# Cross-attention stack on one core: order of the first loads, first q and k by halves, y's statistics ahead of q's scaling, and an earlier folding of v's bias

## Chip, core and metric

The kernel runs on one core of one Trainium2 chip. The metric is the time of one execution in microseconds (us) of the device; a lower time is better. A profile is one execution taken with the hardware profiler; its times count from the first instruction (the span's start).

## What is computed

Sixteen batches of 256 tokens by 256 features (x), with a context y of the same size, go through three attention layers and an MLP, all in float32, with 16 heads of 16 features. Layer 0 is a cross-attention with RMS norms, layer 1 a causal self-attention with rotary embedding, layer 2 a cross-attention with rotary embedding.

```python
# layer 0
q_norm = rmsnorm(query, g_q); c_norm = rmsnorm(context, g_c)
Q = (q_norm @ Wq); K = (c_norm @ Wk); V = (c_norm @ Wv)      # by heads
attn = softmax(where(mask, Q @ K.T * scale, -inf))
x = rmsnorm(query + (attn @ V) @ Wo, g_out)
# layer 1: h = ln(x); q, k rotated; causal; v = h @ sa_wv + sa_bv; x = x + (a @ sa_wo + sa_bo)
# layer 2: q from ln(x), k and v from y;                       x = x + (a @ ca_wo + ca_bo)
# MLP
return x + (gelu(ln(x) @ fc1_w + fc1_b) @ fc2_w + fc2_b)
```

## The kernel before, in words

There are 48 attentions, three layers for each of 16 batches, in the order that `ORDER` lists: the first five are layer 0 of batches 0 to 4. Each attention has four blocks of scores (three in the causal layer): `scores` (L476) makes a block of K times Q in two PSUM tiles `S`, ScalarE takes exp (L487) out of them into `pt`, and `values` (L515) multiplies by V into the one PSUM tile `A` one block later. The preparation of later attentions (statistics, norm, turn, q, k, v) and the finishing of earlier ones (invert, divide, project) is laid between these blocks by hand: everything inside `tc.manual_schedule()` runs in the order in which it is written, on each engine's own queue. What is emitted ahead of that (the memsets, and the two products on zeros at L171) is placed by the framework.

Norms of layer 0 are not applied to the inputs. The gains are multiplied into the weights once (`fold_gain`, L230, on VectorE), x's scale is multiplied into q, and y's scale goes into exp (as `sy`, L343) and into v. `stats_x` and `stats_y` make them: squares with a running sum on VectorE (L246), then two steps on GpSimd (L238, L239). x's scale rx is needed along the free axis; for the first two attentions `spread` (L358) does this by eight small products with the identity, and ScalarE copies the result to `rq` (L363). `q` of layer 0 (L294, then L421) multiplies the product by rq and by a parity column, once for even and once for odd heads, into `qm`. `k` (L294) is copied by ScalarE (L437) to `kT`; `v` (L307) goes out through VectorE (L448) with y's scale and the mask.

Inputs come by DMAs, issued from two queues. SP's takes x's rows, x transposed, y transposed and y's rows of batch 0 (`load_x`, `load_y`), then the mask, batches 1 and 2, and further on all other weights. ACT's takes the vector of small parameters `vec` and then layer 0's Wq, Wk, Wv and Wo. Each of these tiles is 256 KB.

PSUM has eight banks: two tiles S of two banks, one tile A, and three tiles d (`dense_ps`) for all other products.

`fold_v` (L219, L226) makes the product of layer 1's norm bias with its v weights, 16 passes on TensorE, and adds it on VectorE to v's bias row. It and `fold_bias` (L189), the same for q and k and the MLP, stand at the end of the second attention (i == 1, n == 3). The two products on zeros (L171) need only the identity and a zeroed tile, and nothing reads their result.

Of the kernel before, what the change touches and what calls it, by code (L numbers as in the profile page):

```python
# [8 lines left out]
F32 = mybir.dt.float32  # L9
# [3 lines left out]
ALU = mybir.AluOpType  # L13
AX = mybir.AxisListType

P = 128
B, S, D = 16, 256, 256
# [3 lines left out]
KC = D // P  # L21
# [25 lines left out]
def xattn_kernel(  # L47
# [21 lines left out]
    nc = tc.nc  # L69
# [5 lines left out]
    def ctile(shape, name, dtype=F32):  # L75
        return const.tile(shape, dtype, tag=name, name=name)
# [8 lines left out]
    def rows_of(b):  # L85
        return cur[:, NC * b : NC * b + NC, :]
# [4 lines left out]
    yTs = {}  # L91

    def load_x(b):
        nc.sync.dma_start(out=rows_of(b), in_=x[b].rearrange("(c p) d -> p c d", p=P))
        xTs[b] = work.tile([P, KC, S], F32, tag="xT", name=f"xT{b}", bufs=3)
        nc.sync.dma_start(out=xTs[b], in_=xt[b].rearrange("(k p) s -> p k s", p=P))

    def load_y(b):
        yTs[b] = work.tile([P, KC, S], F32, tag="yT", name=f"yT{b}", bufs=Y_LIVE)
        nc.sync.dma_start(out=yTs[b], in_=yt[b].rearrange("(k p) s -> p k s", p=P))  # L100
        ys[b] = work.tile([P, NC, D], F32, tag="y", name=f"y{b}", bufs=3)
        nc.sync.dma_start(out=ys[b], in_=y[b].rearrange("(c p) d -> p c d", p=P))
# [5 lines left out]
    def load_w(t, aps, eng):  # L108
        at = 0
        for a in aps:  # L110
            m = a.shape[1]
            eng.dma_start(out=t[:, :, at : at + m], in_=a.rearrange("(k p) n -> p k n", p=P))
            at += m

    vec = ctile([P, NVEC + 2], "vec")
    nc.scalar.dma_start(out=vec, in_=vecs)
    load_x(0)
    w0_sb = ctile([P, KC, 3 * D], "w0")
    load_w(w0_sb, w0, nc.scalar)
    load_y(0)  # L120
    mask_u8 = ctile([P, B * NC], "mask_u8", U8)
    nc.sync.dma_start(out=mask_u8, in_=mask)
    load(1)
# [36 lines left out]
    def dense_ps():  # L160
        return psD.tile([P, 512], F32, tag="d", name="d")
# [4 lines left out]
        pads.append([ctile([P, 32], f"pad{i}_{j}") for j in range(2)])  # L166
        nc.gpsimd.memset(pads[i][0], 0.0)

    idle = dense_ps()
    for n in range(2):  # L170
        nc.tensor.matmul(  # L171
            idle, lhsT=ident, rhs=firsts[0].rearrange("p t s -> p (t s)"), start=True, stop=True
# [55 lines left out]
    def fold_gain(w, cols, vcol, chunks=range(KC)):  # L228
        for k in chunks:
            nc.vector.tensor_scalar(  # L230
                w[:, k, cols], w[:, k, cols], vec[:, vcol + k : vcol + k + 1], None, ALU.mult
            )
# [52 lines left out]
        )  # L285


    def by_feature(src, w, at):

        ps = dense_ps()  # L290
        for t in range(KC):
            for k in range(KC):
                for j in range(0, P, 32):
                    nc.tensor.matmul(  # L294
                        ps[j : j + 32, t * S : (t + 1) * S],
                        lhsT=w[:, k, at + t * P + j : at + t * P + j + 32], rhs=src[:, k, :],
                        start=(k == 0), stop=(k == KC - 1), skip_group_check=True,
                    )
        return ps.rearrange("p (t s) -> p t s", s=S)
# [15 lines left out]
    class Att:  # L315
# [36 lines left out]
        def spread(self):  # L352

            self.rq = work.tile([P, S], F32, tag="rq", name="rq")
            ps = dense_ps()
            for c in range(NC):
                for j in range(0, P, 32):
                    nc.tensor.matmul(  # L358
                        ps[j : j + 32, c * P : (c + 1) * P],
                        lhsT=self.rx[:, c : c + 1].to_broadcast([P, 32]), rhs=ident,  # L360
                        start=True, stop=True, skip_group_check=True,
                    )
            nc.scalar.copy(self.rq, ps[:, :S])  # L363
# [51 lines left out]
        def q(self):  # L415
            ps = by_feature(self.hT, self.w, 0)
            self.qm = work.tile([P, KC, 2, S], F32, tag="qm", name="qm", bufs=2)
            if self.layer == 0:
                rq = self.rq.unsqueeze(1).to_broadcast([P, KC, S])
                for i in range(2):  # L420
                    nc.vector.scalar_tensor_tensor(  # L421
                        self.qm[:, :, i, :], ps, parity[i], rq, ALU.mult, ALU.mult
                    )
                return
            a, u = self.rotated(ps, 0)
            nc.vector.tensor_tensor(a, a, u, ALU.add)
            for i in range(2):
                nc.vector.tensor_scalar(self.qm[:, :, i, :], a, parity[i], None, ALU.mult)

        def k(self):  # L430
            ps = by_feature(self.kvT, self.w, D)
# [164 lines left out]
    def do(i, *names):  # L596
        a = att(i)
        for name in names:
            if a is not None:
                getattr(a, name)()  # L600
# [242 lines left out]
    combined = combine()  # L843

    with tc.manual_schedule():
        do(0, "stats_x")
        fold_gain(w0_sb, slice(0, D), V_GQ)
        fold_gain(w0_sb, slice(D, 2 * D), V_GC)
        do(0, "turn", "spread", "q", "k", "stats_y")
        fold_gain(w0_sb, slice(2 * D, 3 * D), V_GC)  # L850
        nc.vector.tensor_copy(mask01, mask_u8)
        for va in vas:
# [9 lines left out]
        for i in range(N_ATT):  # L862
            a, last = att(i), att(i - 1)
            ahead = att(i + 3)
            if i > 1 and ahead is not None and ahead.layer == 0:
                load(ahead.b)

            finishing = i >= 3 and att(i - 3).layer == 0  # L870
            for n in range(len(a.blocks)):
                if n == 0 and a.causal and not finishing:
                    do(i + 2, "stats")
                a.scores(n)
                if n > 0:
                    a.values(n - 1)
                elif last is not None:
                    last.values(-1)
                final = len(a.blocks) - 1
                if n == 0:  # L880
                    if i == 0:
                        a.v()
                        do(1, "spread")
                    do(i - 3, "finish")
                    if finishing or not a.causal:
                        do(i + 2, "stats")
                    do(i - 2, "divide")
                    if not finishing:
                        do(i + 2, "norm")
                    do(i + 1, "q")  # L890
                elif n == 1:
                    do(i + 1, "k")
                    if finishing:
                        do(i + 2, "norm")
                    for j in kept.get(i, ()):
                        att(j).keep()
                if n == final - 1:
                    do(i + 1, "v")
                    do(i - 1, "invert")
                    do(i + 2, "send")  # L900
                if n == final:
                    do(i - 2, "project")
                    do(i + 2, "turn", "receive")
                if i == 0 and n == 0:
                    load(4)
                    nc.sync.dma_start(out=bias_sb, in_=rows.partition_broadcast(P))
                    nc.sync.dma_start(out=turn_sb, in_=turn)
                if i == 0 and n == 1:
                    load_w(ca_sb, ca, nc.sync)
                if i == 0 and n == 2:  # L910
                    load_w(fc1_sb, [fc1], nc.sync)
                if i == 1 and n == 0:
                    load_w(sao_sb, [sa_o], nc.sync)
                    load_w(cao_sb, [ca_o], nc.sync)
                if i == 1 and n == 2:
                    load_w(fc2_sb, [fc2], nc.sync)
                    nc.sync.dma_start(
                        out=rope_sb, in_=rope.rearrange("(c p) t d -> p c t d", p=P)
                    )
                if i == 1 and n == 3:  # L920
                    cols = fold_bias()
                    fold_v()
                if i == 2 and n == 3:
                    fold_gain(sa_sb, slice(0, 3 * D), V_G1)
                if i == 3 and n == 3:
                    fold_cols(cols)
                    fold_gain(ca_sb, slice(0, D), V_G2)
                if i in (6, 8) and n == 3:
                    fold_gain(fc1_sb, slice(0, FF), V_G3, [i // 8])
                if n == 1 and i > 8 and not a.causal:  # L930
                    next(combined, None)
                if i == N_ATT - 2 and n == 1:
                    mlps[0].stats()
                    mlps[0].norm()
                if i == N_ATT - 1 and n == 2:
                    mlps[0].turn()
                    mlps[0].mix()
                if i == N_ATT - 1 and n == 3:
                    mlps[1].stats()
                    mlps[1].norm()  # L940
# [472 lines left out]
```

## Time and profile before

| | |
|---|---|
| runs, us | 950.59, 950.79, 953.49; median 950.79 |
| the profiled execution, us | 953.16 |
| its span, us | 951.4 |
| TensorE (PE) busy | 936.1 us, 98% of the span |
| VectorE (DVE) busy | 666.0 us, 70% |
| ScalarE (ACT) busy | 571.9 us, 60% |
| GpSimd (POOL) busy | 294.6 us, 31% |
| DMA | 46.96 MB, 49 GB/s over the span, 333 GB/s from 2 to 12 us |

A busy TensorE is not one at its peak, since matmuls are pipelined and their ends are modelled. In the profile a float32 product shows as two passes, so 16 products are 32 instructions. A wait is put down to what ended last; time of an engine that waits costs something only where it lies in the chain of work that ended last.

### The profile page before, as it was taken

The page shows a single profiled execution, that of the slowest core. Times are in us where ns is not written, and L with a number is a line of the kernel's source. Part 1 is how long each engine was busy: PE and PEld are TensorE (multiplying, and loading weights), DVE is VectorE, ACT ScalarE, POOL GpSimd, SP SyncE. Part 2 cuts the span into 40 slices and gives each one's busy share as a digit, 9 for nine tenths or more (in the row PEclk, how much of TensorE's full clock was granted, in tenths as well). Part 3 has the DMA queues.
Part 4 walks back from the last instruction along what each step waited for, and adds up shares of the span by engine and source line. Part 5 has one row for each costly group of instructions (what it writes and reads, how often), then busy time and mean ns, then how long its engine had stood idle before and what let it go on. Part 6 is the DMA issues. An engine that isn't in the chain of part 4 may idle for free.

```text
span 951.4 us, 30022 instructions
## 1 busy us (share of the span) xinstructions
PE 936.1 (98%) x12374; PEld 551.6 (58%) x12374; DVE 666.0 (70%) x1483; ACT 571.9 (60%) x821; POOL 294.6 (31%) x502
## 2 busy tenths in 40 slices
PE   8999999999999999999999999999999899999997
PEld 4444455445454545455454445445445699999997
DVE  4347768877776797677866768787776776667653
ACT  4666666766666766666766676666676634444440
POOL 4213454334334344144242423334112211222200
PEclk9999999999999999999999999999999999999999
DMA  9531221202121122110222101010101000000001
GB/s 316 171 97 29 78 71 32 71 18 79 25 70 28 42 54 73 24 33 19 72 71 74 32 22 27 19 29 21 26 21 26 13 24 23 13 12 23 23 24 47
DMA packets 66089, 46.96 MB, mean 49 GB/s; under 512 B 25364, under 2 KB 65044, under 8 KB 65944
## 3 DMA queue, kind: packets, MB, share of 16 engines
q1 hardware_dynamic: 64712, 43.89, 16.8%
q8 instruction: 100, 1.64, 0.7%
q10 hardware_dynamic: 1232, 1.07, 0.4%
q14 instruction: 45, 0.37, 0.1%
HBM read 26.54 MB, written 5.79 MB: 34 GB/s over the span
## 4 chain that ended last, share of the span: by engine, by line
PE 88%; DVE 5%; DMA 3%; POOL 1%; ACT 1%; issue 1%; SPq 0%; DVEq 0%; POOLq 0%
PE S L476 18%; PE A L515 17%; PE d L294 16%; PE d L307 15%; PE A L762 6%; PE upX L676 6%; PE downZ L762 3%; PE upZ L676 3%; PE d L274 2%; PE d L762 2%; PE d L676 1%; DMA hop<-av 1%; DVE a L410 1%; PE d L657 1%; DVE u L410 1%
## 5 line engine op out<-in xcount | busy, mean ns | idle before, releaser
L487 ACT ACTIVATE pt<-S 128x1024 f32<-128x1024 f32 x224 | 217.4, 1022 | 114.3 <-PE S L476 114.3
L476 PE MATMUL S<-qm,kT 32*128 32x512 f32 (+1 forms) x1536 | 202.9, 600 | 2.1 <-DVE kT L435 1.0
L515 PE MATMUL A<-pt,va 128*32 128x256 f32 (+1 forms) x3072 | 193.0, 367 | 1.3 <-POOL pt L494 0.8
L515 PEld LDWEIGHTS A<-pt,va 128*32 128x32 f32 x3072 | 80.5, 109 | 158.5 <-issue 95.4
L487 ACT ACTIVATE pt<-S,sy 128x1024 f32<-128x1024 f32 x128 | 135.7, 1111 | 46.1 <-PE S L476 44.0
L555 POOL TENSOR_TENSOR seen<-seen,sums 128x64 f32<-128x64 f32 x48 | 15.4, 320 | 280.4 <-DVE sums L554 185.8
L476 PEld LDWEIGHTS S<-qm,kT 32*128 32x128 f32 x1536 | 62.4, 183 | 68.5 <-issue 25.4
L494 POOL TENSOR_SCALAR_AFFINE_SELECT pt<-pt 128x512 f32<-128x512 f32 x128 | 88.5, 713 | 27.4 <-ACT pt L487 27.3
L283 POOL TENSOR_TENSOR cur<-cur,bias 128x512 f32<-128x512 f32 x48 | 65.3, 1365 | 58.9 <-DVE xn L263 58.9
L402 ACT ACTIVATE a<-d,qk_bias 128x256 f32<-128x256 f32 x128 | 53.8, 471 | 38.5 <-PE d L294 33.4
L294 PE MATMUL d<-hT,sa 128*32 128x256 f32 x1024 | 63.1, 379 | 0.0
L238 POOL TENSOR_SCALAR r_ln<-bmv 128x2 f32<-128x2 f32 x48 | 12.6, 261 | 153.3 <-DVE bmv L257 152.6
L529 ACT COPY av<-A 128x512 f32<-128x512 f32 x96 | 56.6, 590 | 3.5 <-PE A L515 3.2
L410 DVE TENSOR_TENSOR u<-u,turn 128x512 f32<-128x512 f32 x64 | 53.5, 836 | 0.0
L410 DVE TENSOR_TENSOR a<-a,turn 128x512 f32<-128x512 f32 x64 | 50.2, 784 | 2.2
L263 DVE TENSOR_SCALAR xn<-cur,bmv,r_ln 128x256 f32<-128x256 f32 x96 | 51.1, 579 | 0.8 <-POOL r_ln L239 0.6
L707 ACT ACTIVATE g<-g,fb 128x256 f32<-128x256 f32 x96 | 40.9, 497 | 15.4 <-DVE g L700 15.4
L579 DVE TENSOR_TENSOR cur<-d,cur 128x512 f32<-128x512 f32 x32 | 21.7, 679 | 38.8 <-PE d L307 38.7
L406 DVE STREAM_SHUFFLE u<-a 128x512 f32<-128x512 f32 x64 | 47.7, 746 | 0.0
L294 PEld LDWEIGHTS d<-hT,sa 128*32 128x32 f32 x1024 | 34.3, 110 | 22.1
L695 ACT COPY g<-upX 128x512 f32<-128x512 f32 x32 | 17.2, 589 | 46.8 <-issue 39.0
L757 DVE TENSOR_TENSOR g<-g,g 128x512 f32<-128x512 f32 x64 | 40.7, 681 | 0.0
(142 smaller groups left out, 1568.1 us busy)
## 6 DMA issues: line engine op xcount, KB each, us to landing
oT<-av SPq DMA_DIRECT2D x384, 32.0 KB
cur<-in_x SPq DMA_DIRECT2D x16, 256.0 KB
xT<-in_xt SPq DMA_DIRECT2D x16, 256.0 KB
yT<-in_yt SPq DMA_DIRECT2D x16, 256.0 KB
y<-in_y SPq DMA_DIRECT2D x16, 256.0 KB
out<-res SPq DMA_DIRECT2D x15, 256.0 KB
fc<-in_fc SPq DMA_DIRECT2D x2, 1024.0 KB
rq<-rq_hop SPq DMA_DIRECT2D x14, 128.0 KB
```

Source lines behind the costliest of these rows:

```text
L283: nc.gpsimd.tensor_tensor(t, t, bias_sb[:, row : row + D].unsqueeze(1).to_broadcast([P, NC, D]), ALU.add)
L294: nc.tensor.matmul(ps[j : j + 32, t * S : (t + 1) * S], lhsT=w[:, k, at + t * P + j : at + t * P + j + 32], rhs=src[:, k, :], start=(k == ...
L307: nc.tensor.matmul(ps[j : j + 32, c * D : (c + 1) * D], lhsT=src[:, k, c * P + j : c * P + j + 32], rhs=w[:, k, at : at + D], start=(k == ...
L402: nc.scalar.activation(a[:, t], ps[:, t], AF.Identity, bias=bias[:, t : t + 1])
L410: nc.vector.tensor_tensor(t, t, table.unsqueeze(1).to_broadcast([P, KC, S]), ALU.mult)
L476: nc.tensor.matmul(ps[:, j, 2 * m * u : 2 * m * (u + 1)] .rearrange("p (i s) -> p i s", i=2), lhsT=self.kT[r, t, kc * P : (kc + 1) * P], r ...
L487: nc.scalar.activation(pt[:, :, :w], ps[:, :, :w], AF.Exp, scale=scale)
L494: nc.gpsimd.affine_select(out=diag, in_=diag, compare_op=ALU.is_ge, fill=0.0, base=0, pattern=[[0, 2], [0, 2], [1, P]], channel_multiplier=-1,
L515: nc.tensor.matmul(self.av[32 * r : 32 * r + 32, i, q0:S], lhsT=self.va[:, kc, 8 * t + 2 * r + i, :], rhs=pts[r // 2][:, r % 2, i * m : (i ...
L529: nc.scalar.copy(av, self.av)
L676: nc.tensor.matmul(banks[c // 2][:, (c % 2) * S : (c % 2 + 1) * S], lhsT=a[:, c * P : (c + 1) * P], rhs=b, start=(first and c % 2 == 0), s ...
L762: nc.tensor.matmul(ps[:, c, :], lhsT=a[f // 2][:, f % 2, c * P : (c + 1) * P], rhs=b[:, f, :], start=(first and c == 0 and f == 0), stop=True,
```

## The change

1. `load_x` issues x transposed ahead of x's rows, in all batches. Layer 0's weights are loaded one by one: Wq on ACT's queue right after `vec`, Wk on SP's queue after x of batch 0, Wv on SP's after y of batch 0. Wo follows Wq on ACT's queue.
2. Wq's gain is folded ahead of x's statistics.
3. A new method `first_qk` takes the place of `spread`, `q`, `k` and `stats_y` for attention 0: q's product first, then spread, then k in two halves by output features, each in a PSUM tile of its own and copied on its own, then y's statistics, then q's scaling in four instructions of 256 columns instead of two of 512.
4. `spread` uses the PSUM tile A, the two products on zeros one of the tiles S; both used a tile d.
5. `fold_v` moves from the end of the second attention to the end of the first.

In the built program these orders follow. TensorE: q of batch 0, the two products on zeros, spread, k of batch 0, S, v; before: the two products, spread, q, k, S, v. VectorE: Wq's gain, x's squares, Wk's gain, y's squares, qm, Wv's gain; before: x's squares, the gains of Wq and Wk, qm, y's squares, Wv's gain. The order of instructions on GpSimd is the same. Lines move: L171 becomes L174, L294 L297, L219 L222, L358 L361, L476 L495.

```diff
     def load_x(b):
-        nc.sync.dma_start(out=rows_of(b), in_=x[b].rearrange("(c p) d -> p c d", p=P))
         xTs[b] = work.tile([P, KC, S], F32, tag="xT", name=f"xT{b}", bufs=3)
         nc.sync.dma_start(out=xTs[b], in_=xt[b].rearrange("(k p) s -> p k s", p=P))
+        nc.sync.dma_start(out=rows_of(b), in_=x[b].rearrange("(c p) d -> p c d", p=P))
...
     nc.scalar.dma_start(out=vec, in_=vecs)
+    w0_sb = ctile([P, KC, 3 * D], "w0")
+    load_w(w0_sb[:, :, 0:D], w0[0:1], nc.scalar)
     load_x(0)
-    w0_sb = ctile([P, KC, 3 * D], "w0")
-    load_w(w0_sb, w0, nc.scalar)
+    load_w(w0_sb[:, :, D : 2 * D], w0[1:2], nc.sync)
     load_y(0)
+    load_w(w0_sb[:, :, 2 * D : 3 * D], w0[2:3], nc.sync)
...
-    idle = dense_ps()
+    idle = psS.tile([P, 2, 512], F32, tag="S", name="idle")[:, 0]
...
-    def by_feature(src, w, at):
+    def by_feature(src, w, at, ts=range(KC)):
         ps = dense_ps()
-        for t in range(KC):
+        for t in ts:
...
         def spread(self):
             self.rq = work.tile([P, S], F32, tag="rq", name="rq")
-            ps = dense_ps()
+            ps = psA.tile([P, 2, S], F32, tag="A", name="A").rearrange("p i s -> p (i s)")
...
+        def first_qk(self):
+            self.qm = work.tile([P, KC, 2, S], F32, tag="qm", name="qm", bufs=2)
+            self.kT = work.tile([P, KC, S], F32, tag="kT", name="kT", bufs=2)
+            ps = by_feature(self.hT, self.w, 0)
+            self.spread()
+            for t in range(KC):
+                nc.scalar.copy(self.kT[:, t], by_feature(self.kvT, self.w, D, [t])[:, t])
+            self.stats_y()
+            for t in range(KC):
+                for i in range(2):
+                    nc.vector.scalar_tensor_tensor(
+                        self.qm[:, t, i, :], ps[:, t], parity[i], self.rq, ALU.mult, ALU.mult
+                    )
...
     with tc.manual_schedule():
+        fold_gain(w0_sb, slice(0, D), V_GQ)
         do(0, "stats_x")
-        fold_gain(w0_sb, slice(0, D), V_GQ)
         fold_gain(w0_sb, slice(D, 2 * D), V_GC)
-        do(0, "turn", "spread", "q", "k", "stats_y")
+        do(0, "turn", "first_qk")
...
+                if i == 0 and n == 3:
+                    fold_v()
                 if i == 1 and n == 3:
                     cols = fold_bias()
-                    fold_v()
```

## The prediction

> **What bounds the kernel now.** I read the page's chain of work first. TensorE ends it almost everywhere:
>
> ```profile
> PE 88%; DVE 5%; DMA 3%; POOL 1%; ACT 1%; issue 1%; SPq 0%; DVEq 0%; POOLq 0%
> ```
>
> So an edit is worth what it takes out of TensorE's own work, or out of the places where TensorE stands still. Next, TensorE's timeline over the first 18 us (start, length, line, operation, and in brackets the idle time before it):
>
> ```profile
> 1.96 3.78 PE L171 MATMUL d<-first,ident 128*128 128x512 f32 x4 [1.96 <-POOL ident masks.py:199]
> 6.09 0.64 PE L358 MATMUL d<-ident,pad 128*32 128x128 f32 x16 [0.35 <-POOL pad L239]
> 6.55 1.91 PE L294 MATMUL d<-xT,w 128*32 128x256 f32 x32
> 8.28 1.91 PE L294 MATMUL d<-yT,w 128*32 128x256 f32 x32
> 10.89 1.14 PE L476 MATMUL S<-qm,kT 32*128 32x512 f32 x8 [0.70 <-ACT kT L437]
> 11.96 1.93 PE L307 MATMUL d<-w,yT 128*32 128x256 f32 x32
> 14.42 0.64 PE L358 MATMUL d<-ident,pad 128*32 128x128 f32 x16 [0.52 <-POOL pad L239]
> 14.88 1.91 PE L294 MATMUL d<-xT,w 128*32 128x256 f32 x32
> ```
>
> From 14.42 us on (spread of batch 1) TensorE runs without a gap; so the front of the program is judged by when that row starts. It waits for GpSimd's pad L239. Also: L171, the two dummy products on zeros, streams 4 passes of 512 columns, 2048 in all, in 3.78 us; q's L294 streams 32 passes of 256 columns, four abreast, also 2048 in a row, in 1.91. The dummies ran at half pace, q at full pace.
>
> The chain in order of time (start, length, what) shows what leads to 14.42, and the one later stall that the change touches:
>
> ```profile
> 8.61 0.58 DVE qm L421
> 9.28 0.74 DVE qm L421
> ...
> 11.25 0.78 POOL r_y L239
> 12.11 0.19 POOL sy L343
> 12.30 0.93 POOL va L853 x2
> 13.31 0.27 POOL pad L238
> 13.66 0.72 POOL pad L239
> ...
> 25.55 1.13 ACT pt L487
> 26.72 2.13 PE S L476 x8
> ```
>
> Between 26.5 and 28.8 TensorE waits for two exps (the two halves of S L476 start 1.0 us apart): the idle block of the first attention. Last, where v's bias is folded today, in TensorE's timeline:
>
> ```profile
> 42.79 1.05 PE L219 MATMUL d<-sa,vec 128*32 128x256 f32 x16
> 43.77 1.14 PE L476 MATMUL S<-qm,kT 32*128 32x512 f32 x8
> ```
>
> **What the Trainium skill says.** (1) "TensorE: Matmul & The Clock Gate", Part 1: an idle TensorE runs at half clock, and full clock comes after about 4 us of sustained matmuls, give or take 0.5, by a free-running window. The trace agrees: dummies from 1.96 at half pace, spread at 6.09 at full pace, so the grant came 3.8 to 4.1 us after the first matmul. (2) The same page, Part 2: matmuls stay in program order; only weight loads are pulled ahead. The timeline has them in program order. (3) "DMA: Bandwidth & Descriptors", Queues, rings and completion order: each DMA engine takes turns between rings. Here, from 2 to 6 us the queue of SP moved 0.71 MB and that of ACT 0.55 MB, from 6 to 9 us 0.52 and 0.51: about half each while both have work.
>
> **The part that decides: the order on TensorE.** In the built order of the changed kernel TensorE begins with q of batch 0, then the two dummies, then spread, then k; before, the dummies came first. The dummies are no longer a warm-up. They stand in front of spread, on the path.
>
> - q can start when Wq has landed and its first gain is done. Before, the gain (L230) started at 5.08, having waited for Wq, 0.35 a half; Wq keeps its place on ACT's queue and the other ring still moves one 256 KB tile beside it. So q starts at 5.5 us, with no matmul before it: at half pace 2 x 1.73 (its length in the chain) = 3.46, to 8.96.
> - Full clock I take 4.1 us after q's start (as before): 9.6. Of the dummies' 3.46 us at half pace 0.64 is done by then; the other 2.82 take 1.41. They end at 11.0. Bounds: granted at 7.2, half a window's worth earlier, the dummies end near 9.8; granted only at their end, 12.4.
> - spread of batch 0 therefore starts at 11.0, against 6.09. rx has long been ready: Wq's gain is now ahead of x's squares, x's rows come second on SP's ring, at about 5.4 (SP's issue that waited for the second tile before went out at 5.44), squares 5.7 to 6.65, GpSimd 1.1 more, 7.8.
>
> From spread on: rq is copied 1.08 us after spread's start (6.09 to 7.17 before). The four qm of 128x256 follow on VectorE; the row is not in the trace. Half of qm's 0.70 to 0.75 gives 0.37 each; the 128x256 squares L246, 0.42, bound it above. I take 0.37: 1.5 in all, 1.7 at most. Then Wv's gain 0.61, mask 0.1, x's squares of batch 1 0.95, GpSimd's pad 1.2 from the squares' end to TensorE (4.83 to 6.09 before): 1.08 + 0.07 + 1.5 + 0.61 + 0.1 + 0.95 + 1.2 = 5.5. Spread of batch 1 starts at 11.0 + 5.5 = 16.5, 2.1 later than 14.42. TensorE's own path is a little shorter: spread 0.46, k 1.73, S 1.07, v 1.73, 16.0. So the chain moves from POOL's sy and memsets to VectorE: spread, rq, qm, gain, squares. **Front: +2.1 us.**
>
> **The other parts, which this hides or shows.**
> - Loads: y's rows are fifth on SP's ring. Five tiles there and ACT's vec, Wq and Wo make 1.85 MB at some 0.33 MB per us from about 2.2: 7.8, and 0.5 for the last engine, 8.3; their squares began at 9.94 before, behind qm. k's weights at about 6.8 instead of 7.0. Both are early against spread at 11.0: worth nothing. They would count only with the clock warm (first rival). x's transposed tile ahead of its rows in later batches: neither is waited for, 0. The mask, 4 KB, and the next loads wait on older transfers as before, 0.
> - k by halves: kT's first half is copied at spread + 1.95, beside qm. Two copies of 0.37 instead of one of 0.59 on an idle ScalarE. Nothing, unless VectorE's path shrank by 0.4.
> - y's statistics sooner: squares end at about 10.1 at the latest, before rq; sy at 11.6, before S. The 1.5 us that exp waited for sy go, but exp of the first block is not late: its next S comes 2 us after spread of batch 1. The two va memsets are done before the pad needs GpSimd, which is why they leave the chain.
> - **fold_v**: 16 passes, four abreast, 4 rounds of 0.216 = 0.86 us, off the full stretch at 42.79 (the bank that its following S needs is free, exp L487 ended at 42.46) and into the block where TensorE waits at 26.5. There S's first half would start at 27.14 instead of 26.72; the second waits for its exp at 27.72 in any case and the halves use different rows, so the end stays at 28.8. If the halves ran one after the other it costs 0.4. Its add of 0.42 stands on VectorE ahead of the squares of batch 3, which then end some 2 us later than the fold; GpSimd's pad, r_y and va copy behind them are not needed before att 2 (its q's L421 waited for its DMA until 34.0). Its bias row, issued by SP at 19.7, is in before it: SP's stream of 0.37 MB per us brings it by about 27, and the fold moves later with the front. If late, VectorE stands, with more than 5 us of slack. **-0.86 us.**
>
> Sum: 2.1 - 0.86 = +1.2. The profiled execution took 953.16 us (span 951.4, and 1.8 around it): 954.3. The median of the runs shown is 950.79, 2.4 below that execution; the same step on it gives **952.0**. What lies after 45 us keeps its order, and TensorE bounds it.
>
> **Rivals.**
> 1. The new order does no harm: TensorE is at full pace from q on. q takes 1.73, the dummies 1.73, spread of batch 0 starts at 8.96 and that of batch 1 at 8.96 + 5.5 = 14.46, as before; less 0.86 that is 950.0. If the dummies held up nothing either, spread would start at 7.8, qm would wait for y's squares (8.3 + 0.95 = 9.3), and 9.3 + 4.4 = 13.7 is 0.7 early: 949.2, the most that the sooner loads can bring. For it: loads and statistics are in fact sooner. Against it: nothing runs on TensorE before q, and the trace shows that matmuls after an idle start run at half pace.
> 2. Slower than before by over 0.3%: one mechanism, the grant after the dummies. The window is free-running, and 2.85 us more than before need a front delay of 3.7. With q and both dummies wholly at half pace spread starts at 12.4, a delay of 3.4; the rest must come from spread at half pace (0.46 more), so from a grant at about 13 or later, 7.5 us after q's start. At 13.4 it gives 12.4 + 0.46 + 5.5 - 14.42 = 3.9, less 0.86: 953.8. For it: the phase differs by execution. Against it: TensorE is busy without a gap from 5.5, and 4.1 sufficed before.
> 3. The fold is not hidden (halves of S in sequence, or S at 42.79 finds another wait): 0.4 to 0.86 come back, 952.4 to 952.9. Against it: exp and kT are done by then.
>
> **The numbers.** About 0.3%, 2.85 us, is what a measurement of this kernel can tell from no change; the runs shown spread by 2.9. Forecast 0.62; first rival 0.15; second 0.13; third 0.07; 0.03 for a gain beyond 0.3% that I do not see. Within 0.3%: 0.62 + 0.15 + 0.07 = 0.84. The range takes in the first rival's 949.2 and the second's 953.8 with qm at its upper bound (0.2) and the fold's 0.4 on top: 949.2 to 954.4.
>
> **What would show it.** Right: q L297 alone at some 3.5 to 3.8 us, L174 after it, spread of batch 0 near 11, that of batch 1 near 16.4, VectorE ending its wait; the fold between A and S near 28 to 29; no L222 between the bias folds and S. Wrong: q at 1.9 us, spread of batch 0 near 8, or S's start after the fold later than its second exp.

## The result and the profile after

The changed kernel took 954.58 us (median of 22 runs, 952.61 to 957.83); the kernel before, beside it on the same chip, 952.04 (22 runs, 950.08 to 953.49). The ratio is 1.0029 [1.0020, 1.0038]: slower by 2.8 us. (All runs here are in the fast state, and a ratio is worked out from the single runs, so that it differs a little from the quotient of the medians, which gives 2.5 us.) The profiled execution took 953.09 us, span 951.4, which is below its own median, where the one shown of before, 953.16, lies above its own. The two traces therefore end together, and the verdicts come from the times; the traces say what happens where.

The page's chain by engine reads nearly as before (PE 90%, before 88%), so it doesn't show the loss.

TensorE's timeline of the changed kernel, in three cut-outs (start, length, line, operation, idle time before it in brackets):

```profile
5.40 3.64 PE L297 MATMUL d<-xT,w 128*32 128x256 f32 x32 [5.40 <-DVE w L233]
8.97 2.37 PE L174 MATMUL idle<-first,ident 128*128 128x512 f32 x4
11.28 0.64 PE L361 MATMUL A<-ident,pad 128*32 128x128 f32 x16
...
17.13 0.64 PE L361 MATMUL A<-ident,pad 128*32 128x128 f32 x16 [0.55 <-POOL pad L242]
...
28.99 1.05 PE L222 MATMUL d<-sa,vec 128*32 128x256 f32 x16
29.96 1.60 PE L495 MATMUL S<-qm,kT 32*128 32x512 f32 x8
...
45.62 1.14 PE L495 MATMUL S<-qm,kT 32*128 32x512 f32 x8
```

q runs first and at half pace (3.64 us, against 1.91 before), the dummies (the two products on zeros, `idle`) follow it and stand ahead of spread. Spread of batch 0 starts at 11.28 (6.09 before), that of batch 1 at 17.13 (14.42 before): **2.71 us later**. The fold lies in the idle block, and S at 45.62 follows the bias products with no fold between.

The chain in order of time shows what leads from the first spread to the second (start, length, what):

```profile
11.99 0.38 ACT rq L366
...
12.39 0.87 DVE qm L445 x2
...
14.06 0.63 DVE w L233 x2
...
14.78 0.35 DVE sq L249 x2
...
15.67 0.46 POOL pad L241
...
16.20 0.88 POOL pad L242
```

It runs over VectorE, as forecast: qm, Wv's gain, squares, then GpSimd's pad. The memsets and sy have left it.

One thing looks like another cause. In VectorE's timeline of this execution two loads are late:

```profile
9.57 0.61 DVE L233 TENSOR_SCALAR w<-w,vec 128x256 f32<-128x256 f32 x2 [3.14 <-DMA w<-in_w_Wk]
11.07 0.43 DVE L249 SCALAR_TENSOR_TENSOR sq<-y 128x256 f32<-128x256 f32 x1 [0.89 <-DMA y<-in_y]
```

k's weights became usable at 9.57, against 7.01 before, and y's rows at 11.07. Had spread not been late already, these would have held TensorE up. So there are two theories.

### The profile page after: what moved, and what is told of

It reads as the page before. It is cut to its first block, busy times and chain, and to the rows that moved or that the text cites. A ratio compares the mean times of both kernels' runs of the same rounds, so it can differ in the third digit from the quotient of the medians.

```text
span 951.4 us, 30023 instructions
## 1 busy us (share of the span) xinstructions
PE 935.6 (98%) x12374; PEld 552.7 (58%) x12374; DVE 665.9 (70%) x1485; ACT 571.9 (60%) x822; POOL 294.5 (31%) x502
## 4 chain that ended last, share of the span: by engine, by line
PE 90%; DMA 3%; DVE 3%; SPq 1%; POOL 1%; ACT 1%; issue 1%; ACTq 0%; DVEq 0%
PE S L495 18%; PE A L534 17%; PE d L297 16%; PE d L310 15%; PE A L781 6%; PE upX L695 6%; PE downZ L781 3%; PE upZ L695 3%; PE d L277 2%; PE d L781 2%; PE d L695 1%; DMA hop<-av 1%; PE d L676 1%; ACT g L726 1%; DMA rq_hop<-pad 0%
## 5 line engine op out<-in xcount | busy, mean ns | idle before, releaser
L495 PE MATMUL S<-qm,kT 32*128 32x512 f32 (+1 forms) x1536 | 202.6, 600 | 0.2 <-ACT pt L506 0.2
L495 PEld LDWEIGHTS S<-qm,kT 32*128 32x128 f32 x1536 | 62.5, 183 | 65.8 <-issue 26.1
L297 PE MATMUL d<-hT,sa 128*32 128x256 f32 x1024 | 63.4, 379 | 0.0
L297 PEld LDWEIGHTS d<-hT,sa 128*32 128x32 f32 x1024 | 34.7, 110 | 21.8
L589 DVE TENSOR_TENSOR oT<-oT,inv 128x512 f32<-128x512 f32 x48 | 39.7, 828 | 1.6
```

What stands on the lines that cost most here:

```text
L297: nc.tensor.matmul(ps[j : j + 32, t * S : (t + 1) * S], lhsT=w[:, k, at + t * P + j : at + t * P + j + 32], rhs=src[:, k, :], start=(k == ...
L495: nc.tensor.matmul(ps[:, j, 2 * m * u : 2 * m * (u + 1)] .rearrange("p (i s) -> p i s", i=2), lhsT=self.kT[r, t, kc * P : (kc + 1) * P], r ...
```

## The experiments

The main theory: the order on TensorE makes the front late. The dummies have lost their use as a warm-up, q runs cold, and the dummies stand on the path. Its rival: the loads that were reordered now arrive late (theory L), and hold up k and qm. Beside them stood the fold: does its 0.86 us arrive at the end? The runs come in three groups, each on one chip with its own runs of the kernel before (medians 951.98, 952.65 and 953.64, of 46, 48 and 35 runs). Only the runs without dummies leave anything out, and what they leave out is products that nothing reads. *Lag* below is the start of an exp in one trace less the start of the same exp in the trace of before.

### The changed kernel with the dummies first

```diff
+    def warm():
+        idle = psS.tile([P, 2, 512], F32, tag="S", name="idle")[:, 0]
+        for n in range(2):
+            nc.tensor.matmul(
...
     with tc.manual_schedule():
+        warm()
         fold_gain(w0_sb, slice(0, D), V_GQ)
```

> The changed kernel with its two products on zeros written first inside the hand-written order, so that TensorE begins with them again; all else as changed. Theory O (the order on TensorE costs the time: q at half pace, dummies in front of spread): q takes about 1.9 us, spread of batch 0 starts near 8, that of batch 1 near 14 instead of 17.1, and with the fold's 0.86 the kernel is 0.9 to 1.3 us faster than before (ratio 0.9986 to 0.9991). Theory L (the new load order costs it: k's weights landed at 9.5 and y's rows at 11.0 in the changed kernel): spread of batch 0 near 8, but y's squares still end near 12, batch 1's spread starts near 16.5, ratio 1.001 to 1.002.

Measured: 952.56 us, ratio **1.0004 [0.9994, 1.0013]**. TensorE's timeline:

```profile
1.96 3.78 PE L175 MATMUL idle<-first,ident 128*128 128x512 f32 x4 [1.96 <-POOL ident masks.py:199]
5.67 3.01 PE L298 MATMUL d<-xT,w 128*32 128x256 f32 x32
...
15.10 0.64 PE L362 MATMUL A<-ident,pad 128*32 128x128 f32 x16 [0.66 <-POOL pad L243]
```

With all the loads, halves and statistics of the change kept, putting the two products back in front takes spread of batch 1 from 17.13 to 15.10 and the ratio from 1.0029 to 1.0004. So the slowdown comes from the order. The main theory had forecast 0.9986 to 0.9991 and spread of batch 1 near 14; the direction came, a part of the size did not. What is left here, 0.68 us of front, goes with two things in this trace: q still ran partly cold (3.01), and Wv's gain was slow (below).

Theory L falls as the main cause. In this trace y's squares start at 9.04 and Wk's gain at 7.48, with the same list of loads. The changed kernel with the fold put back (below), which has the changed kernel's front as it is, had both loads early too. VectorE's timeline of it:

```profile
7.49 0.62 DVE L233 TENSOR_SCALAR w<-w,vec 128x256 f32<-128x256 f32 x2 [1.03 <-DMA w<-in_w_Wk]
9.07 0.42 DVE L249 SCALAR_TENSOR_TENSOR sq<-y 128x256 f32<-128x256 f32 x1 [0.97 <-DMA y<-in_y]
```

and TensorE's:

```profile
17.25 0.64 PE L361 MATMUL A<-ident,pad 128*32 128x128 f32 x16 [0.44 <-POOL pad L242]
```

Its spread of batch 1 is as late as in the changed kernel, 17.25. The late landing of the changed kernel's profile belongs to that execution (13 of the 16 DMA engines had done their part of Wk at 6.8 us, the last at 9.5).

### The changed kernel without the dummies

```diff
-    idle = psS.tile([P, 2, 512], F32, tag="S", name="idle")[:, 0]
-    for n in range(2):
-        nc.tensor.matmul(
-            idle, lhsT=ident, rhs=firsts[0].rearrange("p t s -> p (t s)"), start=True, stop=True
-        )
```

> The changed kernel without the two products on zeros (nothing reads them). q is still at half pace from 5.4 to 9.0, but spread of batch 0 follows at 9.0 instead of 11.3. Theory O: batch 1's spread 2.0 us or so earlier than 17.1, near 15, kernel near before (ratio 0.9997 to 1.0005). Theory L: qm waits for y's squares (end near 12), batch 1's spread near 16.7, ratio 1.002.

Measured: 953.85 us, ratio 1.0017 [1.0009, 1.0025]. TensorE's timeline:

```profile
5.45 3.64 PE L292 MATMUL d<-xT,w 128*32 128x256 f32 x32 [5.45 <-DVE w L228]
...
15.88 0.64 PE L356 MATMUL A<-ident,pad 128*32 128x128 f32 x16 [0.66 <-POOL pad L237]
```

This splits the loss in two. Dummies in the wrong place cost 0.0012 (1.0029 to 1.0017, about 1.1 us; in the traces spread of batch 1 from 17.13 to 15.88). That q has no warm-up costs a further 0.0013 (1.0017 to 1.0004, about 1.2 us; in the traces 15.88 to 15.10). By the intervals of the ratios each of the two is uncertain by about 1.1 us, so the split says that both parts are there and not which is larger. The main theory had forecast 0.9997 to 1.0005 here and spread of batch 1 near 15. That counted the fold's 0.86 us in full, and in this trace qm had to wait for y's squares (until 10.64) and Wv's gain took 1.22 us.

### The kernel before, with the new order alone

```diff
+        def first_q(self):
+            ps = by_feature(self.hT, self.w, 0)
+            self.qm = work.tile([P, KC, 2, S], F32, tag="qm", name="qm", bufs=2)
+            warm()
+            self.spread()
+            self.k()
...
-        do(0, "turn", "spread", "q", "k", "stats_y")
+        do(0, "turn", "first_q", "stats_y")
```

> The kernel before with one thing of the change: on TensorE q of batch 0 comes first, then the two products on zeros, then spread, then k; q's scaling follows, y's statistics after it; loads, halves and fold as before. Theory O: q at half pace, spread of batch 0 near 11.2, and since y's squares and GpSimd's memsets still stand between qm and the next pad, spread of batch 1 near 18: 3 to 4 us more than before, ratio 1.003 to 1.004. Theory L (the loads cost it): spread of batch 1 near 14.4, ratio 1.000.

The two products use a tile S and spread the tile A here, as in the change.

Measured: 955.28 us, ratio **1.0029 [1.0015, 1.0042]**, that of the whole change. TensorE's timeline:

```profile
9.20 3.10 PE L172 MATMUL idle<-first,ident 128*128 128x512 f32 x4
...
19.11 0.64 PE L359 MATMUL A<-ident,pad 128*32 128x128 f32 x16 [0.79 <-POOL pad L240]
```

The order is enough to make a loss of this size, with every load where it was. The equal ratio is partly luck, since the front is 4.7 us late here and 2.7 in the changed kernel: y's squares and the memsets still stand behind qm, and the clock came later (the dummies took 3.10). That is more than the time shows: the lag is 4.68 at 100 us and 3.31 at 112 us. Something there takes lag up; the fold's runs bear on it.

### The kernel before without its dummies

```diff
-    idle = dense_ps()
-    for n in range(2):
-        nc.tensor.matmul(
-            idle, lhsT=ident, rhs=firsts[0].rearrange("p t s -> p (t s)"), start=True, stop=True
-        )
```

> The kernel before without the two products on zeros: spread at 6.1 and q behind it run at half pace until the clock is granted. By the theory of the order[...] spread takes about 0.4 more and q 1.7 more; k stands ready at 8 but starts near 10.4. Spread of batch 1 near 16.5 and ratio 1.002 to 1.003. If the warm-up is worth nothing there: spread of batch 1 near 14.4, ratio 1.000.

Measured: 954.56 us, ratio 1.0017 [1.0008, 1.0027]. q of batch 0 took 3.32 us there, and spread of batch 1 started at 15.95, 1.53 later. So the warm-up is worth 0.17% (0.08 to 0.27), and the changed kernel lost by its order this and the dummies' time on top.

### The fold alone, and the fold put back

```diff
+                if i == 0 and n == 3:
+                    fold_v()
                 if i == 1 and n == 3:
                     cols = fold_bias()
-                    fold_v()
```

made to the kernel before; and the reverse made to the changed kernel:

```diff
-                if i == 0 and n == 3:
-                    fold_v()
                 if i == 1 and n == 3:
                     cols = fold_bias()
+                    fold_v()
```

> The kernel before with fold_v alone moved to the end of the first attention. Both theories: spread of batch 1 stays near 14.4, the 16 passes lie in the idle block near 26.3, A after S starts at 28.8 as before, and all after 43 us is 0.86 us earlier: ratio 0.9991. If the fold is not hidden there: 0.9995 to 1.0.

> The changed kernel with fold_v back at the end of the second attention. Front as in the changed kernel (spread of batch 1 near 17), then 0.86 us more than the changed kernel: about 2.5 to 3.4 us over before, ratio 1.0026 to 1.0036 or, on the measured 1.0029 of the changed kernel, 1.0038.

Measured: alone 951.92 us, ratio 0.9999 [0.9989, 1.0010]; put back 955.29 us, 1.0032 [1.0019, 1.0045], beside the change's 1.0029. Neither run shows a gain from the fold that stands out of its interval, but neither interval excludes the forecast 0.86 us (0.0009) either. In the trace the gain is there at first: the lag of the fold alone against before goes from +0.22 us ahead of the fold to -0.64 at 46 us, 0.86 as forecast. It is gone by 106 us. TensorE's timeline of before:

```profile
101.40 1.93 PE L307 MATMUL d<-w0o,oT 128*32 128x256 f32 x32 [0.42 <-DVE qm L421]
```

and with the fold alone moved:

```profile
101.52 1.93 PE L307 MATMUL d<-w0o,oT 128*32 128x256 f32 x32 [0.72 <-DVE qm L421]
```

TensorE comes earlier and waits longer: the wait for qm grows from 0.42 to 0.72, one of 0.24 for kT appears at 89.6, and the same row starts at 101.52 instead of 101.40. qm waits on VectorE for rq, which goes out to DRAM and back. That chain was no earlier. The timeline shows the step where it comes loose from TensorE: the softmax sums are stored to DRAM (`hop<-av`) and loaded again in another layout (`sums<-hop`), both issued from SP's queue (SPq). First in before:

```profile
68.24 0.50 SPq L530 DMA_DIRECT2D hop<-av  x1
...
71.70 0.34 SPq L539 DMA_DIRECT2D sums<-hop  x1
...
74.88 0.18 DVE L553 TENSOR_SCALAR sums<-sums 128x32 f32<-128x32 f32 x1 [3.39 <-DMA sums<-hop]
```

and with the fold moved:

```profile
67.27 0.50 SPq L530 DMA_DIRECT2D hop<-av  x1
...
71.85 0.34 SPq L539 DMA_DIRECT2D sums<-hop  x1
...
74.92 0.18 DVE L553 TENSOR_SCALAR sums<-sums 128x32 f32<-128x32 f32 x1 [4.08 <-DMA sums<-hop]
```

The sums came back at the same time though TensorE ran 0.64 us ahead. VectorE waited longer, and what stands behind it on VectorE kept its old time. This is one pair of executions, and chance has a part in it: the store went out 0.97 us earlier, but 4.58 us passed from its issue to that of the reload, against 3.46 before. Over the twelve traces that is 3.1 to 4.6, and 4.58 is the longest.

### The fold's products four times over

```diff
-        for k in range(KC):
+        for k in 4 * list(range(KC)):
```

in the fold of the kernel before, at its old place. It adds three times 0.86 us, 2.6, of pure TensorE time at 43 us and gives the same fold.

> The kernel before, fold_v at its place (end of the second attention), its products made four times over into the same bank: 64 passes instead of 16, 2.6 us more on TensorE near 43 us. If TensorE's work there reaches the end in full, 2.6 us more: ratio 1.0027. If waits further on take it up (which would explain why moving the fold shows no gain in e2, e3 and e5), ratio 1.000 to 1.0015.

Measured: 954.46 us, ratio 1.0013 [1.0002, 1.0024], that is 1.2 us, between 0.2 and 2.3. The full 2.6 us would be 1.0027, outside the interval. TensorE's timeline:

```profile
43.23 3.64 PE L219 MATMUL d<-sa,vec 128*32 128x256 f32 x64
...
103.90 1.93 PE L307 MATMUL d<-w0o,oT 128*32 128x256 f32 x32
```

The row at 103.90 (101.40 before) no longer waits for qm, nor does the A behind it for pt (0.61 in before, at 106.17). The lag is 3.03 us at 100 us and 0.94 at 112, with the 0.44 of its front in both: 2.1 of the 2.6 us are taken up between. But they don't stay away in this execution. By 140 us the lag is 3.83, behind two waits of VectorE for transfers through DRAM: 2.84 us for rq ahead of qm at 132.28, where before has 0.87 at 129.36, and 2.08 us for the sums at 137.31, where before has 0.81 at 133.13.

So the times carry this experiment: less than the full 2.6 us arrives. The trace shows a place where TensorE's delay is absorbed, and also that one execution's trace can't tell how much of it is lost for good. Delays of the front, which move VectorE and the stores as well, fare differently by the trace. Without dummies the kernel before was 1.53 us late at 19 us, 1.53 at 100 and 1.84 at 112, and the changed kernel with the fold put back 2.83, 3.06 and 3.35; but the order alone lost 1.4 of its 4.7 there, and the changed kernel, at 1.85 behind the fold, 0.9. How much arrives of which delay is not settled beyond the times.

### The memsets first

```diff
     with tc.manual_schedule():
+        for va in vas:
+            nc.gpsimd.memset(va[:, :, :, HD:], 1.0)
...
-        for va in vas:
-            nc.gpsimd.memset(va[:, :, :, HD:], 1.0)
```

This came from the run with the dummies first. Its VectorE timeline has, for Wv's gain,

```profile
11.44 1.23 DVE L234 TENSOR_SCALAR w<-w,vec 128x256 f32<-128x256 f32 x2
```

twice the 0.61 that the same step takes in the kernel before, beside two va memsets on GpSimd (11.27, 0.99 us). In the kernel before the memsets stood in the chain ahead of pad. The edit was made to the changed kernel with its dummies first, to the kernel before, and to the kernel before together with the moved fold.

> The changed kernel with the two products on zeros first (as in e1) and, besides, the two va memsets of GpSimd first on its queue. In e1 Wv's gain took 1.23 us beside the memsets, against 0.61 alone. If they hold each other up, the gain is back at 0.61, spread of batch 1 near 14.5 instead of 15.1, ratio 0.9997. If not, as e1: 1.0004.

> The kernel before with only the two va memsets moved to the head of GpSimd's hand-written order, into its idle time from 2.5 to 5 us. They lay in the chain between sy and the pad (0.93 us). Spread of batch 1 starts 0.6 to 1.0 us earlier, 13.4 to 13.8: ratio 0.9990 to 0.9994.

> As e8, and fold_v at the end of the first attention: the version that should beat both kernels. Against e8 another 0.86 us less from 43 us on; ratio 0.9981 to 0.9985. If later waits give the fold's gain back, as e2's 0.9999 leaves possible, ratio 0.999 like e8.

Measured: changed kernel with dummies and memsets first 952.20 us, 0.9992 [0.9980, 1.0003]; kernel before with memsets first 950.72 us, **0.9983 [0.9974, 0.9992]**; the same with the fold moved 951.17 us, 0.9986 [0.9976, 0.9996]. VectorE's timeline of the first of them:

```profile
11.63 0.61 DVE L234 TENSOR_SCALAR w<-w,vec 128x256 f32<-128x256 f32 x2
```

The gain is back at 0.61, and spread of batch 1 starts at 14.68 instead of 15.10. In the kernel before, TensorE no longer waits ahead of that row:

```profile
14.69 0.64 PE L358 MATMUL d<-ident,pad 128*32 128x128 f32 x16
```

Three things follow. The kernel before with this one move beats both kernels, by about 1.6 us its own origin. The fold shows no gain on top of it (0.9986 against 0.9983), as in the runs above. And with the order and the memsets put right, the change's loads, halves and statistics start batch 1 at the same time, 14.68, as the old ones do, 14.69. In time that kernel is not ahead of the old loads with the same fold and memsets, rather behind: 952.20 us (0.9992) against 951.17 (0.9986) on the same chip. The intervals overlap, so a cost of the change's other parts, up to some 1 us, is neither shown nor excluded. The 1.6 us are more than the 0.5 to 0.7 that TensorE waited for pad in the three traces that keep that wait and the warm-up (before 0.52, fold alone 0.56, fourfold 0.70); where the rest comes from is open (the forecast was 0.9990 to 0.9994). The two traces with the memsets moved in the kernel before had a late clock (q at 2.50 and 2.46 us) and a spread of batch 1 no earlier than before's 14.42, so they can't tell.

## Why the prediction was wrong

The direction, and the place and the mechanism of the front's delay, were right. The sum failed: the forecast step was +1.2 us and the measured one 2.8. The excess of 1.6 splits by the prediction's own terms, and a base taken from three runs comes on top.

The step that failed most is the sentence that what lies after 45 us is bounded by TensorE, on which the fold's gain was booked. The chain of before in order of time leaves TensorE at 98 us, for the way of the softmax sums through DRAM and back, and returns to it at 106.94:

```profile
98.00 4.27 DMA hop<-av
...
102.33 2.20 DMA sums<-hop
```

So time taken out of TensorE ahead of this place could not be booked without asking whether the transfer starts earlier too. The terms one by one:

- **The fold, "-0.86 us", booked in full: the largest term that failed.** The fold fits the idle block and costs nothing there in the end. The exp behind it starts 0.53 us later in the run with the fold alone (lag 0.22 to 0.75), but the 0.86 stand in full at 46 us. In the times no gain is seen behind that. By the ratios and their intervals the moved fold is worth -0.1 us, give or take 1.0, alone; +0.3, give or take 1.3, on top of the memsets first; -0.3, give or take 1.5, in the changed kernel against the fold put back. Weighted together that is 0.0, give or take 0.7: the full 0.86 is unlikely, a part of it is not excluded. The traces are divided. Two pairs show the gain gone at 106 us: before and fold alone (lag -0.64 at 85 us, +0.11 at 106), and memsets first without and with the fold (0.27 and -0.62 at 85, -0.35 and -0.12 at 106). The third does not: the changed kernel keeps it against the one with the fold put back (1.85 and 2.83 at 85, 1.28 and 3.69 at 106, -0.44 and 1.53 at the end). What is shown is the fourfold run's time: work added to TensorE alone at this place does not arrive in full. That the waits for DRAM eat the fold's gain is the likeliest account, and not shown.
- **The front, "+2.1 us": 2.71 in the traces.** Spread of batch 0 started at 11.28, not 11.0: the clock was granted 0.3 us later, which is worth half of that, and the dummies were taken at 3.46 us of half pace where the row of before has 3.78. The chain from there took 5.85 us, not 5.5. qm took 1.58 to the gain's start, near the 1.5 taken. The largest miss is pad: 1.55 us from the squares' end to TensorE, where 1.2 was taken from a stretch in which VectorE was otherwise busy. GpSimd's two steps took 0.45 and 0.87 here, 0.23 and 0.71 there. "SBUF — State Buffer" of the Trainium skill, Who interferes with whom, has the rule: a VectorE instruction with two inputs in SBUF contends with a GpSimd instruction that reads SBUF, through a shared port. The trace agrees: the squares of y, a tile multiplied with itself, ran at 15.62 to 16.5, beside both steps.
- **The base.** 950.79 was the median of three runs. Over 22 it is 952.04. That is half of the distance from 952.0 to 954.58, and has nothing to do with the change.
- **The clock at 4.1 us after q's start.** From the paces it came 4.5 us after (the dummies' 2.37 is 0.48 over full pace, so they ran 0.96 us cold: 8.97 + 0.96 = 9.93). The second rival, the grant after the dummies, didn't occur in any of the three traces that have them behind q, but the phase that it rests on does vary, as listed below.
- **Loads, halves, statistics: nothing, right**, in the sense that the right order with the right memsets brings no earlier front than the old loads do. But they weren't quite free, and the times leave room for a small cost (952.20 against 951.17 above). y's squares now stand ahead of qm on VectorE, and with a warm TensorE qm waits for them (9.86 with the dummies first, 8.61 before). The prediction said so for its first rival only.
- **Memsets "done before the pad needs GpSimd"**: right for this kernel; Wv's gain met only their end (0.72 us). With the order put right they run into all of it (1.23).

Front 0.6 and fold 0.86 make 1.5 of the 1.6. This is a reckoning by terms and not a reading of one trace: that of the changed kernel still has the fold's gain at 100 us, its lag falls to 0.93 at 112, and another 1.43 go at 627 us. The latter belongs to the trace of before, which has a wait of 1.01 us for kT there; ten of the eleven other traces gain 1.4 against it at that place. That single executions gain and lose such amounts is why no sum of one trace's waits gives the time, and why the near agreement of 1.5 and 1.6 is in part luck.

## What to carry to other kernels

After an edit to the order of emission, look at the built order of the products that depend on nothing: a warm-up that lands behind real work costs twice, its own time and the cold clock. Where a later stage waits for transfers that another engine feeds, time taken out of TensorE alone can vanish there; look for the next such wait behind an edit, in the chain in order of time, before booking its gain. Take the base from many runs where the step to forecast is of the size of their spread.

## What was not expected of the hardware

- **The grant's time varies more than assumed.** Worked out as above from the last row that runs over its full-pace length, full clock came 3.9 us after the first product (changed kernel without dummies), 4.5 (changed), 4.9 (fold put back), 6.0 (order alone), 3.7 (before without dummies) and, in kernels that begin with dummies at 1.96, at most 4.1 (before), 4.6 (fold alone), 4.9 (fourfold), 5.9 (dummies first), 5.6 and twice 6.1 (memsets first). The Trainium skill's "TensorE: Matmul & The Clock Gate", Part 1, gives about 4 us, give or take 0.5; that holds for four of these twelve traces. It also says that the window is free-running and the cold stretch varies from run to run; the stretch varies here too, but no run here repeats a trace of one kernel. Traces with the same opening lie closer together than that (at most 4.1, 4.6 and 4.9 with before's; 4.5 and 4.9 with the change's; twice 6.1 with the memsets first), so a part may belong to the kernels, and the runs don't separate it from chance. Even with the dummies in front q of batch 0 is partly cold in some traces: 1.91 us in before's, 3.01 with the dummies first.
- **A memset on GpSimd doubled a gain on VectorE**: 0.61 to 1.23 us for two steps of 128x256, in the two traces of the changed form where they meet in full (1.22 without dummies), and 0.61 again with the memsets elsewhere.
- **One load, one late engine**: 256 KB were usable at 9.57 us in one execution and at 7.48 to 8.25 in others of the same list of loads, with 13 of 16 DMA engines done at 6.8.
